# Attention with split operands: the row sum is made with exp, and V's lo part is read from PSUM between two groups of multiplications

## The chip, the cores and the metric

The kernel runs on one core of a Trainium2 chip. The metric is device time in microseconds (us) of one execution. Besides plain runs there is one profiled execution, from which all rows of a profile come. Engines are named PE (TensorE), DVE (VectorE), ACT (ScalarE), POOL (GpSimd) and SP (SyncE, which here only issues DMAs).

## The reference, cut to what matters

One transformer-like block on x of 2 x 2048 x 256, fp32: a layer norm, causal attention without heads, and a gated feed-forward part whose weights are -1, 0 or 1 with a scale; the results of both are added to x.

```
xn = layernorm(x)
q, k, v = xn @ Wq, xn @ Wk, xn @ Wv
scores = where(causal, einsum('bsd,btd->bst', q, k), -max)
attn = softmax(scores * dim_k ** -0.5)
out = x + (attn @ v) @ Wo + ffn(xn)      # ffn: 256 -> 1024 -> 1024 -> 1024 -> 256
```

## The kernel before, in words

**Precision.** An fp32 operand is split into a hi part, rounded to the fp32r format that TensorE multiplies, and a lo part, the rest. A product is hi x hi + hi x lo + lo x hi. Wv and Wo are multiplied together ahead (`wvo`), so V already holds V times Wo; Wq and Wk likewise (`wqk`).

**Tiling.** The sequences are cut into eight blocks of 512 rows, n = 0 to 3 of the first and 4 to 7 of the second. A tile (n, t) is 128 query rows. The 32 tiles run (3,3), (3,2) ... (0,0), then (4,0), (4,1) ... (7,3). Against the key block m a tile needs one score and one weighing; m runs up to n, where only t + 1 parts of 128 keys are wanted.

**`score`** (L344): TensorE multiplies q and k into a PSUM tile `ps` (six multiplications of 512 columns, L359), VectorE copies it to `s` and takes the maximum (L368). After a tile's last block VectorE makes `low`, the negated maximum (L374), ScalarE makes exp in place in pieces of up to 1024 keys with the sum of each piece (L380, `sums`), VectorE transposes 32 x 32 blocks inside 128 rows (L250), and SP stores the result to DRAM (`d`, L255).

**`turn`** (L404) gets P turned over: SP fetches the blocks in their new places (`e`, L262, four DMAs each, two buffers), ScalarE casts them to `pT`'s hi part (L418), and VectorE (even m) or GpSimd (odd m) makes the lo part (L420). Where a piece is short, TensorE transposes instead (L424). `pT` has four buffers and `turn` is written two blocks ahead of the use (`LEAD`).

**`weigh`** (L429): `po`, one PSUM bank of 2 x 256 fp32, gets in one go P's hi times V's hi (`po[:, 0, :]`) and P's hi times V's lo (`po[:, 1, :]`), one multiplication of 512 columns for each 128 keys (L438); then P's lo times V's hi is added to `po[:, 0, :]` with 256 columns each (L443). There are two `po` buffers. After the last block of a tile the sums are added up (L449), inverted (L451), ScalarE takes V's lo part out of PSUM times that (`y`, L453), and VectorE makes `r` = `po[:, 0, :]` x inv + y (L457). Four tiles make one store to DRAM (`r_d`, L462).

**Order.** `merged` (L43) alternates the scores of a tile with the weighing of earlier tiles by their costs; `beside` (L595) scatters in it the looks at the feed-forward weights (L516, L518, L523, L525: do the weights fit the exact ternary path?), which end in `flag` (L687). The framework's scheduler then moves instructions of each engine by its own estimates, and the order it leaves is fixed in the program: each engine works through its own in that order, waiting on semaphores. SP's DMAs too are in one such order. After attention the flag is read and the feed-forward part runs (L736 on), which is TensorE work nearly without gaps.

Of the kernel before, what the change touches and what calls it, by code (L numbers as in the profile page):

```python
# [9 lines left out]
F32 = mybir.dt.float32  # L10
# [4 lines left out]
AF = mybir.ActivationFunctionType  # L15
ALU = mybir.AluOpType
AX = mybir.AxisListType
# [3 lines left out]
P = 128  # L21
TB = 512
NT = TB // P
# [6 lines left out]
UK = 8  # L30
# [32 lines left out]
def attn_ffn_kernel(  # L63
# [35 lines left out]
    nc = tc.nc  # L99
    B, S, D = x.shape  # L100
# [6 lines left out]
    scale = float(wqT.shape[1] * P) ** -0.5  # L107
# [45 lines left out]
    with ExitStack() as actx:  # L153
# [3 lines left out]
        rp = actx.enter_context(tc.tile_pool(name="rp", bufs=2))  # L157
# [6 lines left out]
        small = actx.enter_context(tc.tile_pool(name="small", bufs=4))  # L164
# [82 lines left out]
        def turn_blocks(src, k, name):  # L247

            b = bp.tile([P, UK * P], F32, tag="b", name=f"b_{name}")[:, : k * P]
            nc.vector.transpose(  # L250
                b.rearrange("p (g k q) -> p k g q", g=P // Q, q=Q),
                src.rearrange("p (k g q) -> p k g q", g=P // Q, q=Q),
            )
            d = dram.tile([P, k * P], F32, name=f"d_{name}")
            nc.sync.dma_start(out=d, in_=b)  # L255
            return d
# [87 lines left out]
        def score(n, t, m, order):  # L344
            first = n - n % NB
            if m == order[0]:
                state[n, t] = {
                    "s": sp.tile([P, S], F32, tag="s", name=f"s_{n}_{t}"),
                    "tops": small.tile([P, NB], F32, tag="tops", name=f"tops_{n}_{t}"),
                    "sums": small.tile([P, NB], F32, tag="sums", name=f"sums_{n}_{t}", bufs=9),  # L350
                }
            st = state[n, t]
            w = TB if m < n else (t + 1) * P
            at = (m - first) * TB
            ps = ps_s.tile([P, TB], F32, tag="ps", name=f"pss_{n}_{t}_{m}")
            k = 0
            for c in range(DC):
                for a, b in ((0, 0), (0, 1), (1, 0)):
                    nc.tensor.matmul(  # L359
                        out=ps[:, :w], lhsT=qs[n][:, c, a, ts(t, P)], rhs=ks[m][:, c, b, :w],  # L360
                        start=(k == 0), stop=(m < n and k == 3 * DC - 1),
                    )
                    k += 1
            if m == n:
                nc.tensor.matmul(
                    out=ps[:, ds(w - P, P)], lhsT=ident_r, rhs=mask_r, start=False, stop=True
                )
            marks["DVE"] = nc.vector.tensor_scalar(  # L368
                st["s"][:, ds(at, w)], ps[:, :w], 1.0, None, ALU.mult, ALU.max,
                accum_out=st["tops"][:, m - first : m - first + 1],  # L370
            ).ins
            if m == order[-1]:
                low = small.tile([P, 1], F32, tag="low", name=f"low_{n}_{t}")
                nc.vector.tensor_reduce(  # L374
                    low, st["tops"][:, : n - first + 1], AX.X, ALU.max, negate=True
                )
                kt = (n - first) * NT + t + 1
                for u in range(0, kt, UK):
                    at = ds(u * P, min(UK, kt - u) * P)
                    marks["ACT"] = nc.scalar.activation(  # L380
                        st["s"][:, at], st["s"][:, at], AF.Exp, bias=low,
                        accum_out=st["sums"][:, u // UK : u // UK + 1],
                    ).ins
                for u in range(0, kt, UK):
                    k = min(UK, kt - u)
                    if by_blocks(n, t, first + u // NT):
                        d = turn_blocks(st["s"][:, ds(u * P, k * P)], k, f"{n}_{t}_{u}")
                        units.append((n, t, u, k, d))

        units, fetched = [], {}  # L390

        def by_blocks(n, t, m):
            kt = (n % NB) * NT + t + 1
            u = (m % NB) * NT // UK * UK
            return min(UK, kt - u) >= LEAST and (n, t) != (N - 1, NT - 1)
# [33 lines left out]
        def weigh(n, t, m):  # L429
            first = n - n % NB  # L430
            st = state[n, t]
            if m == first:
                st["po"] = ps_o.tile([P, 2, D], F32, tag="po", name=f"po_{n}_{t}")
            tiles = NT if m < n else t + 1
            pT = st.pop(m)

            for j in range(tiles):
                nc.tensor.matmul(  # L438
                    out=st["po"], lhsT=pT[:, 0, ts(j, P)], rhs=vs[m][:, j, :, :],
                    start=(m == first and j == 0), stop=False,  # L440
                )
            for j in range(tiles):
                nc.tensor.matmul(  # L443
                    out=st["po"][:, 0, :], lhsT=pT[:, 1, ts(j, P)], rhs=vs[m][:, j, 0, :],
                    start=False, stop=(m == n and j == tiles - 1),
                )
            if m == n:
                total = small.tile([P, 1], F32, tag="total", name=f"total_{n}_{t}")
                nc.vector.reduce_sum(total, st["sums"][:, : (n - first) * NT // UK + 1], axis=AX.X)  # L449
                inv = small.tile([P, 1], F32, tag="inv", name=f"inv_{n}_{t}")  # L450
                nc.vector.reciprocal(inv, total)  # L451
                y = rp.tile([P, D], F32, tag="y", name=f"y_{n}_{t}")
                nc.scalar.activation(y, st["po"][:, 1, :], AF.Copy, scale=inv)  # L453
                if n not in attn:
                    attn[n] = rp.tile([P, NT, D], F32, tag="r", name=f"r_{n}"), []
                r, made = attn[n]
                nc.vector.scalar_tensor_tensor(  # L457
                    r[:, t, :], st["po"][:, 0, :], inv, y, ALU.mult, ALU.add
                )
                made.append(t)  # L460
                if len(made) == NT:
                    nc.sync.dma_start(out=r_d[n], in_=r.rearrange("p t d -> p (t d)"))  # L462
                del state[n, t]

        def score_steps(n, t):
            order = list(range(n - n % NB, n + 1))
            return [
                (6 * (TB if m < n else (t + 1) * P), lambda m=m: score(n, t, m, order))
                for m in order
            ]  # L470

        def weigh_steps(g, until):

            steps = []
            while g < len(blocks) and blocks[g][0] <= until:
                while turned[0] <= min(g + LEAD, len(blocks) - 1) and (
                    turned[0] <= g or blocks[turned[0]][0] <= until + 1
                ):
                    b = blocks[turned[0]]
                    steps.append((0 if by_blocks(*b[1:]) else 2 * TB, lambda b=b: turn(*b[1:])))  # L480
                    turned[0] += 1
                _, n, t, m = blocks[g]
                steps.append((6 * TB if m < n else 6 * P * (t + 1), lambda b=blocks[g]: weigh(*b[1:])))
                g += 1
            return g, steps
# [43 lines left out]
        sums = xh0.rearrange("p c h t -> p (c h) t")  # L529
# [79 lines left out]
        queries(NB - 1, 1)  # L609
        order = list(range(NB - 1, -1, -1))  # L610
        score(NB - 1, NT - 1, NB - 1, order)
        wvo = weights_product("wvo", raw["v"], raw["o"], 1.0)
        for n in order[1:]:
            keys(n)
            score(NB - 1, NT - 1, n, order)
            for half in range(2):
                values(n + 1, half)
# [5 lines left out]
        tiles = [divmod(i, NT) for i in range(NB * NT - 1, -1, -1)]  # L623
# [37 lines left out]
        j = -1  # L661
# [460 lines left out]
```

## Time and profile before

| | us |
|---|---|
| Median of 3 runs | 874.41 (873.32 to 876.95) |
| The profiled execution, its own time | 872.97 |
| Its span, first to last instruction | 871.1 |
| PE busy | 851.1 (98%) |
| DVE, ACT, POOL busy | 630.3, 498.2, 236.3 |
| Attention on PE | until 276.9 of the span |

A busy share is the mean over stages. In a row of the costliest groups one reads line, engine, operation, tiles, shape and count, then busy time, mean ns of one, and the idle time ahead of it with what ended it. DMAs in flight don't show as busy time of an engine.

### The profile page before, as it was taken

The page shows a single profiled execution, that of the slowest core. Times are in us where ns is not written, and L with a number is a line of the kernel's source. Part 1 is how long each engine was busy: PE and PEld are TensorE (multiplying, and loading weights), DVE is VectorE, ACT ScalarE, POOL GpSimd, SP SyncE. Part 2 cuts the span into 40 slices and gives each one's busy share as a digit, 9 for nine tenths or more (in the row PEclk, how much of TensorE's full clock was granted, in tenths as well). Part 3 has the DMA queues.
Part 4 walks back from the last instruction along what each step waited for, and adds up shares of the span by engine and source line. Part 5 has one row for each costly group of instructions (what it writes and reads, how often), then busy time and mean ns, then how long its engine had stood idle before and what let it go on. Part 6 is the DMA issues. An engine that isn't in the chain of part 4 may idle for free.

```text
span 871.1 us, 12211 instructions
## 1 busy us (share of the span) xinstructions
PE 851.1 (98%) x4280; PEld 720.7 (83%) x4280; DVE 630.3 (72%) x1127; ACT 498.2 (57%) x881; POOL 236.3 (27%) x176
## 2 busy tenths in 40 slices
PE   8999999999989999999999999999999999999996
PEld 5888888988877878888988888988888898888886
DVE  5699688786873995985496596569478648848663
ACT  2547555755644665677266486536657635657670
POOL 4112633201111473540143150025024012402401
PEclk8999999999999999999999999999999999999999
DMA  9867599866792979743424444443444432144412
GB/s 322 312 230 226 176 326 300 298 230 212 243 324 93 375 280 336 273 146 143 139 87 150 146 144 145 149 127 103 145 145 145 146 139 97 49 145 146 145 49 77
DMA packets 63845, 162.51 MB, mean 187 GB/s; under 512 B 6560, under 2 KB 36384, under 8 KB 54560
## 3 DMA queue, kind: packets, MB, share of 16 engines
q1 hardware_dynamic: 58304, 145.92, 48.4%
q10 hardware_dynamic: 5472, 15.73, 5.6%
q8 instruction: 36, 0.59, 0.3%
q14 instruction: 33, 0.27, 0.1%
HBM read 120.21 MB, written 47.71 MB: 193 GB/s over the span
## 4 chain that ended last, share of the span: by engine, by line
PE 61%; DMA 3%; POOL 1%; DVE 1%; issue 0%; SPq 0%; DVEq 0%; POOLq 0%
PE ps_h_X L780 26%; PE ps_h_Z L780 13%; PE ps_w_B L736 10%; PE ps_h_Y L780 7%; PE ps_y L918 6%; DMA stgt_h<-in_ffn_h_w 1%; DMA w_h_S<-factors_h 1%; POOL sums_h L151 1%; DVE f_w_B L762 0%; DMA rt<-r_d 0%; POOL rt L908 0%; DVE h_B L720 0%; DMA out<-yt 0%; POOL f_w_B L761 0%; DVE f_w_B L742 0%
## 5 line engine op out<-in xcount | busy, mean ns | idle before, releaser
L359 PE MATMUL pss<-k,q 128*128 128x512 f32 (+3 forms) x480 | 110.4, 368 | 2.1 <-DVE q L210 1.1
L359 PEld LDWEIGHTS pss<-k,q 128*128 128x128 f32 x480 | 81.6, 189 | 14.9 <-DVE q L210 1.4
L780 PE MATMUL ps_h_X<-h_h_T,w_h_S 128*128 128x512 f32 x384 | 89.1, 389 | 0.3 <-DMA w_h_S<-factors_h 0.3
L780 PEld LDWEIGHTS ps_h_X<-h_h_T,w_h_S 128*128 128x128 f32 x384 | 72.0, 188 | 15.6 <-ACT k_h_u L801 0.7
L438 PE MATMUL po<-v,pT 128*128 128x512 f32 x272 | 79.0, 403 | 3.7 <-ACT pT L418 2.8
L420 POOL TENSOR_TENSOR pT<-e,pT 128x512 fp32r<-128x512 f32 (+3 forms) x30 | 35.6, 1188 | 161.6 <-ACT pT L418 111.0
L908 POOL TENSOR_TENSOR rt<-rt,xt 128x1024 f32<-128x1024 f32 x8 | 19.6, 2453 | 209.9 <-DMA rt<-r_d 209.9
L801 ACT ACTIVATE k_h_u<-k_h_u,h_s_sb 128x512 f32<-128x512 f32 x64 | 46.3, 724 | 41.1 <-DVE k_h_u L800 40.9
L741 ACT ACTIVATE f_w_B<-ps_w_B,w_s_sb 128x512 f32<-128x512 f32 x64 | 43.0, 684 | 43.5 <-PE ps_w_B L736 43.5
L918 PEld LDWEIGHTS ps_y<-w_sbt,h_h_B 128*128 128x128 f32 x512 | 62.0, 192 | 0.3
L918 PE MATMUL ps_y<-w_sbt,h_h_B 128*128 128x256 f32 x512 | 62.1, 283 | 0.0
L736 PE MATMUL ps_w_B<-xh,w_sb 128*128 128x512 f32 x256 | 59.5, 390 | 1.3 <-DVE r L457 1.3
L418 ACT CAST pT<-e 128x512 fp32r<-128x512 f32 (+3 forms) x60 | 32.6, 574 | 48.9 <-DMA e<-d 31.0
L780 PE MATMUL ps_h_X<-h_h_T,w_h_A 128*128 128x512 f32 x256 | 59.3, 389 | 0.0
L780 PE MATMUL ps_h_Y<-h_h_B,w_h_A 128*128 128x512 f32 x256 | 59.3, 389 | 0.0
L736 PE MATMUL ps_w_B<-xh1t,w_sb 128*128 128x512 f32 x256 | 58.7, 389 | 0.0
L438 PEld LDWEIGHTS po<-v,pT 128*128 128x128 f32 x272 | 48.6, 192 | 11.6 <-ACT pT L418 3.3
L736 PEld LDWEIGHTS ps_w_B<-xh,w_sb 128*128 128x128 f32 x256 | 47.8, 188 | 11.2 <-issue 1.5
L780 PEld LDWEIGHTS ps_h_Y<-h_h_B,w_h_A 128*128 128x128 f32 x256 | 48.0, 188 | 10.0
L780 PEld LDWEIGHTS ps_h_X<-h_h_T,w_h_A 128*128 128x128 f32 x256 | 48.0, 188 | 10.0
L736 PEld LDWEIGHTS ps_w_B<-xh1t,w_sb 128*128 128x128 f32 x256 | 48.0, 188 | 10.0
L380 ACT ACTIVATE s<-s,low 128x1024 f32<-128x1024 f32 (+7 forms) x48 | 43.0, 897 | 20.3 <-DVE low L374 19.9
(139 smaller groups left out, 1846.7 us busy)
## 6 DMA issues: line engine op xcount, KB each, us to landing
w_h_S<-factors_h SPq DMA_DIRECT2D x32, 1024.0 KB, 4.7
w_h_A<-factors_h SPq DMA_DIRECT2D x24, 1024.0 KB, 4.7
d<-b SPq DMA_DIRECT2D x18, 512.0 KB, 4.2
e<-d SPq DMA_DIRECT2D x72, 128.0 KB, 4.1
xT_d<-k SPq DMA_DIRECT2D x8, 1024.0 KB, 7.5
stg<-in_ffn_h_w ACTq DMA_DIRECT2D x16, 512.0 KB, 6.6
x<-in_attn_x SPq DMA_DIRECT2D x16, 256.0 KB, 5.5
r_d<-r SPq DMA_DIRECT2D x8, 512.0 KB, 5.3
```

Source lines behind the costliest of these rows:

```text
L151: engine.tensor_tensor(sums[:, i, :], x, y, op)
L359: nc.tensor.matmul(out=ps[:, :w], lhsT=qs[n][:, c, a, ts(t, P)], rhs=ks[m][:, c, b, :w], start=(k == 0), stop=(m < n and k == 3 * DC - 1),)
L380: marks["ACT"] = nc.scalar.activation(st["s"][:, at], st["s"][:, at], AF.Exp, bias=low, accum_out=st["sums"][:, u // UK : u // UK + 1],).ins
L418: nc.scalar.copy(hi, src)
L420: engine.tensor_tensor(lo, src, hi.bitcast(F32), ALU.subtract)
L438: nc.tensor.matmul(out=st["po"], lhsT=pT[:, 0, ts(j, P)], rhs=vs[m][:, j, :, :], start=(m == first and j == 0), stop=False,)
L736: nc.tensor.matmul(out=p, lhsT=w[:, c, ts(o, P)], rhs=xh[:, c, a, :], start=(c == 0 and a == 0), stop=(c == DC - 1 and a == 1),)
L741: nc.scalar.activation(f, p1, AF.Silu, scale=sc["w1"][:, o : o + 1])
L780: nc.tensor.matmul(out=out[o], lhsT=w[:, c, ts(o, P)], rhs=sets[right][c][:, a, :], start=(start and c == 0 and a == 0), stop=(c == HK - 1 ...
L801: nc.scalar.activation(C[k][o], r[o] if r else banks[o], AF.Gelu, scale=s[:, at : at + 1])
L908: nc.gpsimd.tensor_tensor(rest, rest, xt, ALU.add)
L918: nc.tensor.matmul(out=ys[t][:, :D], lhsT=h[c][:, a, ts(t, P)], rhs=w3_sb[:, c, :], start=(c == 0 and a == 0), stop=(c == HC - 1 and a == 1),)
```

## The change

The sum over the pieces and its reciprocal are written in `score`, right behind a tile's exp and block transposes, and the reciprocal is kept with the tile's state in one of nine buffers. In `weigh`, at the last block of a tile, ScalarE's y is written between the hi multiplications and the lo multiplications of that block, where it was written after both. The framework tracks `po` as one tile, so the lo multiplications that follow y in the text wait until y has been read. Both groups of multiplications get `skip_group_check=True`, since the bank is read while its accumulation is open. r stays the last step. As the scheduler places instructions anew, their order on every engine differs in the whole of attention; what is computed does not.

```diff
@@ score
                         units.append((n, t, u, k, d))
+                total = small.tile([P, 1], F32, tag="total", name=f"total_{n}_{t}")
+                nc.vector.reduce_sum(total, st["sums"][:, : (kt - 1) // UK + 1], axis=AX.X)
+                st["inv"] = small.tile([P, 1], F32, tag="inv", name=f"inv_{n}_{t}", bufs=9)
+                nc.vector.reciprocal(st["inv"], total)
@@ weigh
             for j in range(tiles):
                 nc.tensor.matmul(
                     out=st["po"], lhsT=pT[:, 0, ts(j, P)], rhs=vs[m][:, j, :, :],
-                    start=(m == first and j == 0), stop=False,
-                )
+                    start=(m == first and j == 0), stop=False, skip_group_check=True,
+                )
+            if m == n:
+                y = rp.tile([P, D], F32, tag="y", name=f"y_{n}_{t}")
+                nc.scalar.activation(y, st["po"][:, 1, :], AF.Copy, scale=st["inv"])
             for j in range(tiles):
                 nc.tensor.matmul(
                     out=st["po"][:, 0, :], lhsT=pT[:, 1, ts(j, P)], rhs=vs[m][:, j, 0, :],
-                    start=False, stop=(m == n and j == tiles - 1),
+                    start=False, stop=(m == n and j == tiles - 1), skip_group_check=True,
                 )
             if m == n:
-                total = small.tile([P, 1], F32, tag="total", name=f"total_{n}_{t}")
-                nc.vector.reduce_sum(total, st["sums"][:, : (n - first) * NT // UK + 1], axis=AX.X)
-                inv = small.tile([P, 1], F32, tag="inv", name=f"inv_{n}_{t}")
-                nc.vector.reciprocal(inv, total)
-                y = rp.tile([P, D], F32, tag="y", name=f"y_{n}_{t}")
-                nc.scalar.activation(y, st["po"][:, 1, :], AF.Copy, scale=inv)
                 if n not in attn:
                     attn[n] = rp.tile([P, NT, D], F32, tag="r", name=f"r_{n}"), []
                 r, made = attn[n]
                 nc.vector.scalar_tensor_tensor(
-                    r[:, t, :], st["po"][:, 0, :], inv, y, ALU.mult, ALU.add
+                    r[:, t, :], st["po"][:, 0, :], st["inv"], y, ALU.mult, ALU.add
                 )
```

## The prediction

> **What bounds the kernel now.** I read the busy shares first, then TensorE's own waits, the windows around its largest hole, the timeline there, and last the tile `po` that the change works on.
>
> ```profile
> PE 851.1 (98%) x4280; PEld 720.7 (83%) x4280; DVE 630.3 (72%) x1127; ACT 498.2 (57%) x881; POOL 236.3 (27%) x176
> ```
>
> TensorE bounds. Only its holes, or work added to it, move the end. Its waits, from the list of who waited for whom (engine, line, releaser: us in total, times, longest):
>
> ```profile
> PE po L438 <- ACT pT L418: 2.8, 1, 2.8
> ...
> PE ps_w_B L736 <- DVE r L457: 1.3, 1, 1.3
> ...
> PE po L438 <- DVE r L457: 0.9, 1, 0.9
> ```
>
> The windows (stretch, length, busy us of each engine, then TensorE's granted clock, DMA share, GB/s) divide attention from 53 us on:
>
> ```profile
> 53.00:240.00 187.00, 183.72 (x1029) 159.28 (x1028) 154.81 (x403) 113.03 (x228) 52.95 (x50) 1.00 0.77 249
> ...
> 257.20:261.00 3.80, 1.05 (x10) 0.81 (x8) 2.03 (x5) 1.89 (x5) 0.00 (x0) 0.98 0.88 279
> 261.00:264.50 3.50, 3.46 (x11) 2.93 (x12) 1.58 (x5) 2.48 (x5) 1.44 (x2) 0.54 0.33 91
> 264.50:278.20 13.70, 12.42 (x76) 10.68 (x74) 5.06 (x9) 4.67 (x9) 1.89 (x2) 1.00 0.05 14
> ```
>
> TensorE stands idle for 3.3, 2.75 and 1.3 us, and after the hole at 258 its clock is 0.54 for 3.4 us, worth 1.7 us. These 9 us are all that a better order inside attention could win. The feed-forward part after 278 us keeps its instructions. Now `po` (min/median/max ns) and who let ScalarE wait before y:
>
> ```profile
> L453 ACT ACTIVATE y<-po,inv x32: 452/469/489, 73.1 to 276.9; 128x256 f32<-128x256 f32 x32
> L457 DVE SCALAR_TENSOR_TENSOR r<-po,inv,y x32: 438/475/486, 76.4 to 277.4; 128x256 f32<-128x256 f32 x32
> ...
>   PE po L443: 14.2, 9
> ```
>
> Only before 9 of 32 y's did ScalarE sit waiting for TensorE. At most others y was late, because ScalarE was behind. One such place in the timeline of tile (2,2), whose last `po` multiplication started at 116.11:
>
> ```profile
> 116.11 0.52 PE L443 MATMUL po<-v,pT 128*128 128x256 f32 x3
> ...
> 120.45 1.06 ACT L523 ACTIVATE stg<-stg 128x1024 f32<-128x1024 f32 x1 [1.23 <-DMA stg<-in_ffn_h_w]
> 121.41 0.46 ACT L453 ACTIVATE y<-po,inv 128x256 f32<-128x256 f32 x1
> ```
>
> Pairing each y with its `po` in the timeline, y starts between 0.04 and 4.8 us after the last multiplication of its tile. Nobody on TensorE cares today.
>
> **What the Trainium skill says.** "PSUM — Partial Sum Buffer", Terms, calls simultaneous access by TensorE and ScalarE to one bank and quadrant an error. `po` is one whole bank of 512 fp32, so a y read between hi and lo must hold lo back; in the built program each last lo group indeed waits for ScalarE. No run here shows the collision. "TensorE: Matmul & The Clock Gate", Architectural detail, calls ScalarE and VectorE strict FIFO; the y above, ready at 116.7 and started at 121.4 behind other work, agrees. The same page, Part 1, halves the clock after about one idle window of 3.4 us; here 2.8 us of idle were followed by 0.54.
>
> **The change, part by part.**
>
> *Sum and reciprocal with exp.* 32 x (114 + 153) ns = 8.5 us of VectorE stay. In both built programs each sum stands right after its tile's last block transpose, which waits for the same exp; on the tiles without transposes it stands near where it stood. Only the reciprocal moves, past one to six VectorE instructions. No TensorE wait hangs on it. Cost: 0. If the cover went (a sum blocking VectorE on a late exp), it would show as the 1.1 us in 3 waits that these sums have now, doubled: +1 us at most.
>
> *y before lo.* Same 32 activations and 544 `po` multiplications. What is new is 32 waits: lo of a tile's last block waits for y, y for the hi group and for everything ahead of it on ScalarE. Behind lo, on TensorE, everything queues. From the timeline, spacings are 0.227 us (512 columns), 0.12 (256) and 0.11 (128). A wait with nothing between hi and lo costs: end of the last hi 0.39 us after its start, handover 0.05, y 0.47, handover 0.05 = 0.96 instead of 0.23, so 0.73 us. The built order leaves three tiles so: (7,0), (7,1), (7,3). In the other 29, other multiplications stand between, 2.0 to 7.1 us by those spacings, median about 4.3. Bounds for these 29: below, 0, y always in time. Above, adding to each tile today's lateness of y and 1 us for lo, y and handovers, eight tiles exceed their cover, by 9.4 us together. But in the new order ScalarE's y stands ahead of work that it stood behind (at (2,3) two passes of 1.05 us, at (2,2) an exp of about 1 us and a pass that had waited for a DMA), so most of that lateness goes. What remains is casts that wait for their transfer (31.0 us in 16 waits, 1.9 each): if four of them outlast their cover by 0.5 us, +2 us. I take +2.
>
> *What the later lo moves.* The pT ring has four buffers, so a last block's pT is freed later, the casts behind it come later, the e buffers (two) are read later, and SP's fetches into them start later. SP's queue shows it: at the end e_1_0, e_1_8, e_2_0 and e_2_8 all stand behind the last d stores and the flag's load stands ahead of e_2_0; before, e_1_0 stood ahead of those stores and the flag behind every fetch. I walked this tail from E, the end of score (7,3),5, with 29.4 us of multiplications left. Before, 276.9 - 29.4 - 4.7 of stalls puts E at 242.8.
> - TensorE reaches lo of (7,0),4 at E+8.7. Its VectorE subtraction stands behind the mask of the last w3 tile (L516). That load took 7.0 us (251.88 to 258.9); issued at E+2.1 it ends at 9.1, then 0.69 + 0.69: E+10.5. TensorE waits 1.9.
> - That subtraction frees e for e_1_0: issued at 10.5, before at 244.61, E+1.8. Its second half stands behind the store of r, which waits for the subtraction, a weight look (1.25), another subtraction and r: last issue 13.8, landing 4.1 later (median of these fetches), cast 0.62: (7,1),4 starts at 18.5. TensorE, with y of (7,0) uncovered, is there at 15.5: 3.0 idle.
> - e_2_0 waits for GpSimd's subtraction of (7,1),5 (20.4), last issue 21.9, 2.3 to land (the quiet-queue value), cast: 24.8. TensorE arrives at 24.1. e_2_8 then fits.
> - From 24.8: 5.2 + 5.6 + 0.9 of multiplications and transposes and 0.7 for (7,3): E+37.2 against 34.1. Afterwards r follows lo without y, -0.5.
> Sum 2.6; with part of a half-clock phase after the 3.0 us hole, +3. Ends: -4.5 (hole and phase gone) to +7 (each fetch 2 us slower).
>
> *Sum.* 0 + 2 + 3 = +5 us. The profiled execution took 872.97 (span 871.1 and 1.9 around it), hence 878; the median of the runs is 1.4 above that, hence 879.4.
>
> **Rivals.**
> - *Hidden anyway.* ScalarE is 57% busy, the order puts 4 us between hi and lo, and the many waits of TensorE on casts and subtractions in 53 to 240 us leave only 3.3 us idle. Then only the three uncovered y's remain (0.73 twice, and 0.73 - 0.5 at the end, where r no longer waits for y), less about 1 us of the present hole: 874.4 + 1.5 + 0.2 - 1 = 875. Against: the tail's fetches stand visibly later.
> - *The tail gets shorter* (faster). In the new order 8 us more multiplications follow the last scores: at the point that has 17.8 us left before, the new one has 26. If DMAs return quickly (2.3 us each, the w3 load within 5), (7,1),4 finds its cast nearly ready, the 2.75 us hole and the 1.7 us of half clock go, and r is quicker by 0.5: 874.4 - 4.9 = 869.5. It decides where e_1_0 has landed by E+14.
> - *ScalarE sets the pace.* Casts that wait for e, exp that waits for VectorE's maxima (15.9 us in 12 waits), then y: the full 9.4 of shortage with the tail: 874.4 + 9.4 + 5 = 889. It needs y to stay as late as today.
> - *The change does nothing, as the sums stand where they stood.* True of the sums; the lo waits are in the built program.
>
> **Chances.** Slower by lo's waits and tail 0.46 (own range 877 to 884), ScalarE's pace 0.07, hidden 0.33, shorter tail 0.14. About 0.5% (4.4 us) is what a measurement here tells from no change. So slower 0.53, same 0.33, faster 0.14. The range 870 to 886 drops about half of the shorter tails and the slowest of the pace cases.
>
> **What would show it.** Right: L443 waiting for ScalarE's y at several places, about 0.7 us each at (7,0), (7,1); holes of 2 to 3 us before `po` L438 near E+15, waiting for ScalarE's cast, itself for e; VectorE waiting for the stg load ahead of it; span about 876. Wrong: no PE wait on y at all, TensorE busy without a hole from 240 to 278, or granted clock 1.00 throughout the tail. The prediction fails if the new order's DMA traffic lands faster than today's, or if an earlier stretch loses or gains several us that I took as unchanged.

## The result, and the profile after

| | before | after |
|---|---|---|
| Median, timed side by side | 873.66 us | 879.43 us |
| Ratio, 95% interval | | 1.0076 (1.0053 to 1.0099) |
| The profiled execution, its span | 872.97, 871.1 | 878.6, 876.7 |
| Feed-forward part begins (first multiplication into `ps_w_B`) | 278.16 | 283.15 |
| From there to the end | 592.9 | 593.6 |

The change makes the kernel 0.76% slower; the forecast was 879.4 us. The forecast's sum was right for a reason that was only half right: of its two losses one was hardly there, and the other was larger.

Here as in the prediction (7,1),4 stands for tile (7,1) against key block 4, and e_1_0 for the buffer into which SP fetches the turned blocks of tile (7,1) for its first 1024 keys (e_1_8: the rest). In the kernel after, lines are numbered a little higher: the cast to `pT` is L422, the subtraction L424, hi of `po` L443, lo L451, y L449, r L459, the mask of a weight look L518, the first feed-forward multiplication L738. TensorE's busy share and its waits, which answer to those shown of before (engine, line, releaser: us in total, times, longest):

```profile
PE 854.5 (97%) x4280; PEld 721.7 (82%) x4280; DVE 630.7 (72%) x1127; ACT 498.3 (57%) x881; POOL 236.0 (27%) x176
```

```profile
PE po L443 <- ACT pT L422: 2.8, 3, 1.6
PE po L451 <- DVE pT L424: 1.8, 1, 1.8
PE po L451 <- ACT y L449: 1.8, 3, 0.7
...
PE ps_w_B L738 <- DVE r L459: 0.8, 1, 0.8
```

The second and third lines are new: lo waits once for a subtraction on VectorE, and three times for y. The first was one hole of 2.8 us and is three smaller ones. The windows, with the columns as before:

```profile
53.00:240.00 187.00, 184.23 (x1020) 159.45 (x1019) 156.23 (x410) 112.35 (x224) 49.05 (x49) 0.99 0.78 256
242.00:250.00 8.00, 8.00 (x44) 6.81 (x43) 5.33 (x17) 4.45 (x9) 1.36 (x1) 1.00 1.02 353
250.00:262.00 12.00, 8.05 (x39) 6.45 (x38) 5.58 (x10) 4.73 (x10) 2.44 (x2) 0.83 0.41 125
262.00:284.00 22.00, 19.83 (x102) 16.09 (x103) 7.34 (x11) 6.97 (x14) 5.48 (x4) 0.94 0.19 50
```

The last two stretches before, the second up to the feed-forward part:

```profile
250.00:262.00 12.00, 9.21 (x49) 7.79 (x48) 7.68 (x20) 6.79 (x13) 2.38 (x3) 0.95 0.92 271
262.00:278.20 16.20, 14.92 (x84) 12.78 (x82) 5.93 (x11) 6.15 (x13) 2.69 (x3) 0.93 0.10 29
```

From 53 to 240 us TensorE is as busy as before (184.2 of 187 us, before 183.7). The loss lies behind 250: 4 idle us in 12 and a clock of 0.83 (before 2.8 and 0.95), then 2.2 idle us (before 1.3). The tile `po`:

```profile
L449 ACT ACTIVATE y<-po,inv x32: 453/473/483, 72.1 to 281.0; 128x256 f32<-128x256 f32 x32
L459 DVE SCALAR_TENSOR_TENSOR r<-po,inv,y x32: 442/476/487, 79.0 to 282.4; 128x256 f32<-128x256 f32 x32
...
  PE po L443: 17.0, 7
```

Now ScalarE sits waiting for the hi group before 7 of 32 y's, before it was 9: ScalarE is still late at most tiles. But at 29 of them TensorE has something else to do. To place the loss, both traces were read at the same point of TensorE's work. With 29.3 us of multiplications left before the feed-forward part (the point E of the prediction) before stands at 242.6 us and after at 242.9. From there to the feed-forward part it takes 35.6 us before and 40.3 after: 4.7 of the 5.6 us between the spans are in this tail, 0.3 ahead of it and 0.6 behind. A second profile of the kernel after (span 879.9) agrees on the place: of 8.8 us above before 7.6 are in the tail.

The tail in the timeline of TensorE, after (start, us, engine, line, operation, count, then idle time and releaser):

```profile
253.37 0.74 PE L451 MATMUL po<-v,pT 128*128 128x256 f32 x4 [1.84 <-DVE pT L424]
...
259.82 0.36 PE L451 MATMUL po<-v,pT 128*128 128x256 f32 x1 [0.54 <-ACT y L449]
261.75 2.07 PE L443 MATMUL po<-v,pT 128*128 128x512 f32 x4 [1.57 <-ACT pT L422]
...
268.67 0.47 PE L451 MATMUL po<-v,pT 128*128 128x256 f32 x2 [0.66 <-ACT y L449]
...
281.57 0.74 PE L451 MATMUL po<-v,pT 128*128 128x256 f32 x4 [0.56 <-ACT y L449]
283.15 1.16 PE L738 MATMUL ps_w_B<-xh,w_sb 128*128 128x512 f32 x4 [0.84 <-DVE r L459]
```

The three y's are those of (7,0), (7,1) and (7,3), the three that the built order had left uncovered. The idle times are 6.0 us here and 4.05 before (2.75 and 1.3): 2.0 of the 4.7. The y's add 1.8 and the subtraction 1.8, while the hole ahead of (7,1),4 is 1.2 shorter than before's and the last wait for r 0.4. TensorE's clock was at half from 254.5 and from 261.3, for 3.4 us each, before only once, from 260.8: 1.7. The remaining 1.0 is put down to what each of the four additional stops costs beside its idle time (behind a stop four multiplications of 512 columns take 1.20 us, otherwise 1.09); it was not measured apart.

What was late ahead of this, in the timelines of ScalarE, VectorE, GpSimd and SP, after:

```profile
246.75 1.16 ACT L380 ACTIVATE s<-s,low 128x1024 f32<-128x1024 f32 x1 [3.55 <-DVE low L374]
...
249.03 0.60 ACT L422 CAST pT<-e 128x512 fp32r<-128x512 f32 x1
```

```profile
250.95 0.69 DVE L518 TENSOR_SCALAR stg<-stg 128x1024 uint32<-128x1024 uint32 x1 [1.44 <-DMA stg<-in_ffn_w_w]
251.56 1.76 DVE L424 TENSOR_TENSOR pT<-e,pT 128x512 fp32r<-128x512 f32 x1
```

```profile
251.18 1.59 POOL L424 TENSOR_TENSOR pT<-e,pT 128x512 fp32r<-128x512 f32 x1 [7.39 <-ACT pT L422]
```

```profile
243.81 10.35 SPq L262 DMA_DIRECT2D e<-d  x6
256.89 0.34 SPq L464 DMA_DIRECT2D r_d<-r  x1
257.27 10.03 SPq L262 DMA_DIRECT2D e<-d  x14
```

ScalarE waited 3.55 us for the negated maximum of the last tile, (7,3), then took its exp, and only then, at 249.03, cast the first block of (7,0), which stood behind it. So the lo part of (7,0),4 came late on VectorE, and e came free late for e_1_0. Its first two fetches are the last two of the row of six, issued at 253.38; the store of r stands next in SP's queue, and the other two fetches came behind it from 257.27. The last of the four had landed at 261.0, 18.1 us past E. Before, e_1_0 had landed at 252.2, 9.7 past E.

One more thing is in these lines. The subtraction at 251.56 took 1.76 us where such a one takes 0.69, and GpSimd's subtraction ran until 252.77. The Trainium skill, "SBUF — State Buffer", SBUF: two separate sides, says that VectorE and GpSimd share a pair of ports under an exclusive lock, and that a VectorE operation with two SBUF inputs waits for a GpSimd operation on SBUF that started first. The trace agrees: the four VectorE subtractions of 512 columns with both inputs in SBUF that began with 0.8 to 1.2 us of a GpSimd subtraction to go took 1.38 to 1.76 us, and each ended 0.55 us behind GpSimd's; most others took 0.67 to 0.69. So of the 1.84 us wait above an estimated 1.07 (1.76 less 0.69) belongs to this lock and not to the mask that the prediction named.

### The profile page after: what moved, and what is told of

Read it like the earlier page. It is cut to its first block, busy times and chain, and to the rows that moved or that the text cites. A ratio compares the mean times of both kernels' runs of the same rounds, so it can differ in the third digit from the quotient of the medians.

```text
span 876.7 us, 12246 instructions
## 1 busy us (share of the span) xinstructions
PE 854.5 (97%) x4280; PEld 721.7 (82%) x4280; DVE 630.7 (72%) x1127; ACT 498.3 (57%) x881; POOL 236.0 (27%) x176
## 4 chain that ended last, share of the span: by engine, by line
PE 61%; DMA 3%; POOL 1%; DVE 1%; issue 0%; SPq 0%; DVEq 0%; POOLq 0%
PE ps_h_X L782 26%; PE ps_h_Z L782 12%; PE ps_w_B L738 10%; PE ps_h_Y L782 7%; PE ps_y L920 6%; DMA stgt_h<-in_ffn_h_w 1%; DMA w_h_S<-factors_h 1%; POOL sums_h L151 1%; DVE f_w_B L764 0%; DMA rt<-r_d 0%; POOL rt L910 0%; DVE h_B L722 0%; DMA out<-yt 0%; POOL f_w_B L763 0%; DVE f_w_B L744 0%
## 5 line engine op out<-in xcount | busy, mean ns | idle before, releaser
L443 PE MATMUL po<-v,pT 128*128 128x512 f32 x272 | 79.0, 405 | 3.7 <-ACT pT L422 2.8
L424 POOL TENSOR_TENSOR pT<-e,pT 128x512 fp32r<-128x512 f32 (+3 forms) x30 | 36.7, 1225 | 159.7 <-ACT pT L422 80.3
L738 PE MATMUL ps_w_B<-xh,w_sb 128*128 128x512 f32 x256 | 59.5, 390 | 0.8 <-DVE r L459 0.8
L738 PE MATMUL ps_w_B<-xh1t,w_sb 128*128 128x512 f32 x256 | 58.7, 389 | 0.0
L443 PEld LDWEIGHTS po<-v,pT 128*128 128x128 f32 x272 | 48.8, 193 | 11.8 <-ACT pT L422 3.3
L738 PEld LDWEIGHTS ps_w_B<-xh,w_sb 128*128 128x128 f32 x256 | 47.8, 188 | 10.8 <-issue 1.0
L738 PEld LDWEIGHTS ps_w_B<-xh1t,w_sb 128*128 128x128 f32 x256 | 48.0, 188 | 10.1 <-issue 0.2
L763 POOL TENSOR_TENSOR k_h_u<-k_h_p,k_h_u 128x512 f32<-128x512 f32 x16 | 24.3, 1522 | 109.8 <-ACT h_h_B L721 97.4
```

Source lines behind the costliest of these rows:

```text
L424: engine.tensor_tensor(lo, src, hi.bitcast(F32), ALU.subtract)
L443: nc.tensor.matmul(out=st["po"], lhsT=pT[:, 0, ts(j, P)], rhs=vs[m][:, j, :, :], start=(m == first and j == 0), stop=False, skip_group_che ...
L738: nc.tensor.matmul(out=p, lhsT=w[:, c, ts(o, P)], rhs=xh[:, c, a, :], start=(c == 0 and a == 0), stop=(c == DC - 1 and a == 1),)
L763: nc.gpsimd.tensor_tensor(B["B12"][i], B["B22"][i], B["B12"][i], ALU.subtract)
```

## The experiments

The theory after the comparison: the loss is in the tail, by the later order of casts and fetches and by y's without cover. The rival: y between hi and lo costs something at every tile, through 32 waits of lo. Another: any new order on the engines costs a few us by chance. Later one more stood against these: that the transfers beside the 1 MB load of xh are what is late. In the lists below "above before" is against runs of the kernel before on the same chip.

**One half of the change: sums early, y behind lo.**

```diff
@@ weigh (against the kernel after)
-            if m == n:
-                y = rp.tile(...); nc.scalar.activation(y, st["po"][:, 1, :], AF.Copy, scale=st["inv"])
             for j in range(tiles):
                 nc.tensor.matmul(out=st["po"][:, 0, :], ...)
             if m == n:
+                y = rp.tile(...); nc.scalar.activation(y, st["po"][:, 1, :], AF.Copy, scale=st["inv"])
```

> The sum and the reciprocal stand in score as in the changed kernel, y stays behind both groups of multiplications as before; the sixteen other tiles of the order hardly move. Late-tail theory (the lo groups held back by y free the pT buffers late, so the last fetches of e start late): no change, 873.7 within 1.5, with one hole of about 2.8 us ahead of po near the end as before. Rival of the waits on y: no change either. Rival of the shuffle (any new order on the engines costs a few us by chance): 875 to 879.

Measured: 874.35 us, before 872.9, ratio 1.0024 (1.0006 to 1.0043). This is in the range of the late tail and under that of chance. The order of the tail is that of before (the last scores stand where they stood), and its hole is 2.3 us. The early sums alone cost 0.1 to 0.4%. The profiled execution (872.6, 1.8 under the median of these runs) has a tail 2.3 us longer than before's, of which 0.6 is idle time and 1.7 a second half-clock phase. One execution does not tell whether the loss lies there: its place stays open.

**The other half: y early, sums back in the weighing.**

```diff
@@ score
-                total = ...; nc.vector.reduce_sum(total, ...); st["inv"] = ...; nc.vector.reciprocal(st["inv"], total)
@@ weigh, behind hi
             if m == n:
+                total = ...; nc.vector.reduce_sum(total, ...); st["inv"] = ...; nc.vector.reciprocal(st["inv"], total)
                 y = rp.tile([P, D], F32, tag="y", name=f"y_{n}_{t}")
```

> The kernel after, with sum and reciprocal back in the weighing, just ahead of y, which stays between hi and lo. Nothing is left out. Theory: the place of the sums is worth nothing and y between hi and lo is the whole loss: 4.5 to 7 us above before, TensorE waiting for y at the three tiles of block 7. Rival: making the sums early is what the y needs to be in time, and without it y comes later at more tiles: TensorE waits for y at more than three tiles and the time is 8 us or more above before. Other rival: with this kernel's order of the tail (4 us less of multiplications behind the last scores than in the kernel after) the tail loses less: 2 to 4 us above before.

Measured: 873.7 us, before 875.16, ratio 0.9997 (0.9983 to 1.0011): no loss. All three expectations missed, the last by the least. All 32 y's stand between hi and lo here, and TensorE waits for two of them (0.4 us at 136.6, 0.56 at (7,3)). Its waits:

```profile
PE po L439 <- ACT pT L418: 3.9, 3, 2.3
...
PE po L451 <- DVE pT L420: 1.0, 1, 1.0
...
PE po L451 <- ACT y L449: 1.0, 2, 0.6
```

What differs is the order that the scheduler left. Two lines of ScalarE and one of SP:

```profile
251.07 0.30 ACT L418 CAST pT<-e 128x128 fp32r<-128x128 f32 x1 [2.20 <-DVE low L374]
251.28 1.15 ACT L380 ACTIVATE s<-s,low 128x1024 f32<-128x1024 f32 x1
```

```profile
247.86 1.94 SPq L262 DMA_DIRECT2D e<-d  x4
```

The exp of (7,3), which begins at 251.28, stands behind all casts of (7,0), of which the first line is the last, and the four fetches of e_1_0 go out together at 247.86. They have landed 12.9 us past E, and the tail takes 35.9 us, as before (it idles 1.0 us more than before's and has no half-clock phase). So y ahead of lo need not cost anything, and a new order need not either. With both halves together the scheduler puts the last scores, with their exp, ahead of work that the tail needs sooner: in the kernel after 8.7 us more of multiplications are left behind those scores than before, here 4.7. But this kernel's order differs from both others in all of attention, so the run does not single out the place of that exp.

**y early in all blocks but the last.**

```diff
@@ weigh, behind hi (and y behind lo for the others)
-            if m == n:
+            if m == n and n < N - 1:
```

> The changed kernel, but in the last query block, tiles (7,0) to (7,3), y goes back behind lo. The order at the end is that of the changed kernel: 27.9 us of multiplications left at the last score, the fetches e_0_8 to e_2_8 behind the last stores of d. No multiplication of block 7 waits for y. Late-tail theory: most of the loss stays, +3.5 to +4.5 against before, 877 to 878.5, with the hole ahead of (7,1),4. Rival of the waits on y: the 1.8 us of waits and what they bring are gone, 874 to 875.5.

Measured: 876.95 us, before 872.9, ratio 1.0045 (1.0025 to 1.0064). The 4 us above before are in the range of the late tail. With 28 early y's and the order of the kernel after, TensorE waits for no y at all, so in this profile those 28 have no direct cost. Its hole at (7,1),4 became larger instead:

```profile
PE po L443 <- ACT pT L422: 5.1, 2, 3.8
```

The three uncovered y's of block 7 are worth about 0.3%, 2 to 2.5 us, of the loss (the interval of the kernel after, 1.0053 to 1.0099, overlaps this one). The rest stays, and the largest wait of the tail is the hole before the casts of e_1_0, which here had landed 16.6 us past E.

**y early in the last block alone**, the other way round.

```diff
-            if m == n:
+            if m == n and n == N - 1:
```

> y ahead of lo only in tiles (7,0) to (7,3), sums in score. The order at the end is that of before: 19.2 us left at the last score, e_1_0 ahead of the last stores of d. Late-tail theory: close to before, 873.7 to 875.2, the waits on y at most 0.7 us each at one or two places. Rival of the waits on y: 875.5 to 877, since the same last tiles wait for y as in the changed kernel.

Measured: 875.6 us, ratio 1.0032 (1.0015 to 1.0048), 2.7 us above before. One y is waited for (0.6 us), the hole for the casts is 2.1. Its profiled execution has half clock in another place too (at 125.9 us for 3.4 us), behind a wait of the scores on VectorE's q (1.7 us). The time lies in the range of the rival and not in that of the late tail: for the late tail this is a miss. But one wait of 0.6 us for y is not what the rival counted on. The order here is nearly that of the run with the early sums alone, and the two ratios (1.0024 and 1.0032) are not told apart, so what the early sums cost may be all of it.

**The kernel after with one look less**, so that VectorE does not wait for the last w3 tile. The second half of w3 isn't looked at, which leaves out one mask, one pass and its part of the flag.

```diff
@@ the looks at w3
-            if c >= 2:
+            if c == 2:
```

> The changed kernel without the look at the second half of w3 (its load, the mask on VectorE, the sum on ScalarE are left out; the flag then does not cover those weights). It takes away what VectorE waits for ahead of the subtraction of (7,0),4. Late-tail theory: the chain of fetches starts up to 1.8 us earlier and one half-clock phase less, so 2 to 4 us faster than the changed kernel, 875.5 to 877.5. Rival: the fetch is bound by e's readers on GpSimd anyway, then at most 1 us.

Measured: 879.29 us, ratio 1.0077 (1.0048 to 1.0106): nothing gained, a miss for the late tail and in the range of the rival. The wait of lo of (7,0),4 was gone, and TensorE came to (7,1),4 3.9 us earlier, at 256.3, but there it stood 2.4 us longer:

```profile
260.25 2.07 PE L443 MATMUL po<-v,pT 128*128 128x512 f32 x4 [3.95 <-ACT pT L422]
```

It then ran 6.8 us at half clock where after had 3.4 twice. So the stall on the mask was not on the path that sets the end. VectorE's subtraction took 1.77 us here as well, beside GpSimd's, and e_1_0 could go out only 0.56 us earlier, at 252.82.

**The store of r one weighing later**, so that all of e_1_0 stands ahead of it in SP's queue.

```diff
@@ weigh, last block of a tile
+                for w in held: w()
+                held.clear()
-                    nc.sync.dma_start(out=r_d[n], in_=r.rearrange("p t d -> p (t d)"))
+                    held.append(lambda n=n, r=r: nc.sync.dma_start(out=r_d[n], in_=...))
+                    if n in (0, N - 1): held.pop()()
```

> The kernel after, with the store of a block of r written one weighing later, so that in SP's queue all four fetches of e_1_0 stand ahead of it (and two or three of e_1_8). Nothing is left out. Theory, the late tail: in the kernel after, the second half of e_1_0 was issued at 257.27, 3.5 us after the first half, because the store of r stood between and r was made only at 256.37; it landed at 260.7 and the cast, at 261.08, let TensorE wait 1.57 us and then run 3.4 us at half clock. Without the store between, the second half is issued near 254.5 and lands near 257, ahead of TensorE: the hole before (7,1),4 and its half clock go, 1.6 + 1.7 = 3.3 us, so 2 to 3.5 us faster than after: 2.5 to 4 us above the kernel before. Rival: GpSimd's subtraction and the d loads set the landing of the whole e_1 group and the hole stays: within 1 us of after, 5.5 to 6.5 above before.

Measured: 879.21 us, before 875.16, ratio 1.0051 (1.0028 to 1.0073), 4.05 us above before: just outside the range of the theory, under that of the rival. The mechanism is there: e_1_0 lands 15.4 us past E instead of 18.1, and the hole shrinks from 1.57 to

```profile
258.13 1.20 PE L443 MATMUL po<-v,pT 128*128 128x512 f32 x4 [0.59 <-ACT pT L422]
```

The profiled tail takes 38.4 us, 1.9 less than after; but that execution is the fastest of the seven, 3.3 us under their median. By the times alone it isn't told from after, as the intervals overlap.

**The load of xh behind the last fetch of e**, in the kernel before and in the kernel after.

```diff
@@ fetch_blocks
-                nc.sync.dma_start(out=e[ts(g, Q), :]...)
+                marks["SP"] = nc.sync.dma_start(out=e[ts(g, Q), :]...).ins
@@ after the attention loop
-        nc.sync.dma_start(out=xh0...)
+        with tc.issue_after(marks["SP"]):
+            nc.sync.dma_start(out=xh0...)
```

> The kernel before, with the load of xh (the 1 MB that the feed-forward part starts with) issued behind the last fetch of e instead of at 241.7 us. Nothing is left out. Theory, transfers share the DMA engines: in the kernel before the e fetches issued at 244.6 beside xh landed 6 us later, and those issued at 262.3 in a quiet queue 2 us later. With xh gone the fetches and the w3 load of 244 to 258 land 2 to 4 us earlier, the hole of 2.75 us at 258 and its half clock (1.7 us) go or shrink: 1.5 to 4.5 us faster than the kernel before. Rival: the waits are those of the order (e buffers, subtractions, SP's queue) and not of the transfers' length: within 1 us of before.

> The kernel after, with the same move of the load of xh behind the last fetch of e; the scheduler then also puts the store of r behind all of e_1_0, as in the run with the later store. Nothing is left out. Theory, the late tail made of both the transfers' length and the store in SP's queue: the 1.84 us wait of lo of (7,0),4 on the subtraction behind the mask of w3 (whose load landed at 250.95 beside xh) and the 1.57 us hole at (7,1),4 both go, with both phases of half clock; what stays are the three uncovered y's: 4 to 6.5 us faster than after, 0 to 2 above before. Rival: only the order of lo counts (pT and e buffers come free too late): 0 to 2 us faster than after.

Measured: in the kernel before 875.06 us against 875.16, ratio 1.0008 (0.9991 to 1.0024): nothing. In the kernel after 877.46, ratio 1.0033 (1.0017 to 1.0049), 2.3 us above before. The first answers the question of the transfers: in the order of before the 1 MB beside the fetches doesn't set the time (the hole was 2.75 us before; the profile of this run, 3.2 us above its median, has two, of 3.0 and 1.8). The second, between its two expectations, gave back more than half of the loss, though here the scheduler also put the store of r behind all of e_1_0. The hole at (7,1),4 was still 1.70 us; the wait of (7,0),4 on VectorE was gone, and 0.55 us on GpSimd had come in its place.

**The exp of the last tile behind the casts of (7,0) and the first of (7,1)**, one edge of order more in the kernel after; and that kernel again beside it.

```diff
@@ turn
-                nc.scalar.copy(hi, src)
+                marks["CAST"] = nc.scalar.copy(hi, src).ins
@@ score
+                    with tc.issue_after(marks["CAST"]) if (n, t) == (N - 1, NT - 1) else nullcontext():
                         marks["ACT"] = nc.scalar.activation(st["s"][:, at], st["s"][:, at], AF.Exp, ...)
```

> The kernel after with one order edge more: ScalarE's exp of the last tile, (7,3), is kept behind the casts of (7,0) and the first of (7,1), where the scheduler had put it ahead of all casts of (7,0). Sums, y and lo stay as in the kernel after, and the last scores stand as early in TensorE's order. Nothing is left out. Theory, the order on ScalarE: in the kernel after ScalarE stood 3.55 us before that exp, waiting for VectorE's low, and then took 2.3 us for it, with the casts of (7,0) queued behind; so e was freed for e_1_0 at 253.4, 10.5 us after the last score of 512 columns before (E), against E+1.8 to E+5.2 in the kernel before and in the one with late sums, which lose nothing. With the exp behind the casts e_1_0 is issued by E+6, the wait on VectorE's subtraction (1.84) and the hole at (7,1),4 (1.57) go with their half clock, y of (7,0) is covered again: 4 to 6.5 us faster than after, 0 to 2 us above before. Rival: the loss comes from y standing in the way of lo and of the pT ring, and the exp's place is worth nothing: within 1.5 us of after, 5 to 7 above before.

> The kernel after, unchanged, timed beside the run with the last exp later. Both theories: 5.8 us above before (ratio 1.005 to 1.010), spans by the profile 874 to 878, as runs of one kernel differ in how much half clock the start has.

Measured: with the edge 877.01 us, ratio 1.0050 (1.0033 to 1.0067); after again 880.23, ratio 1.0069 (1.0041 to 1.0097); before 873.64. So 3.2 us of 6.6 came back by the medians, and 1.7 of 6.0 by the ratios, whose intervals overlap. The time lies between the theory and the rival. The kernel after was again as slow as expected; its profiled span, 879.9, was above the expected 874 to 878. The profile with the edge shows why only part came back. The first fetch of e_1_0 went out 6.8 us past E instead of 10.5, and all four landed by 11.2 instead of 18.1, sooner than in the kernel that loses nothing; the wait on VectorE's subtraction in the tail was gone. Not all of that is the exp's: the scheduler here also put the store of r behind these fetches, as in the run with the later store. And the moved exp is late for someone else: TensorE transposes P of (7,3) itself and stood for it,

```profile
255.79 1.09 PE L430 MATMUL pt<-ident,s 128*128 128x128 f32 x8 [0.86 <-ACT s L382]
```

and two y's of block 7 (0.66 and 0.56 us in its tail) were still uncovered.

**That edge and xh's load last.**

> The run with the last exp later, and with the load of xh behind the last fetch of e. Nothing is left out. If what is left of the tail's hole is the length of the transfers beside xh: 1 to 3 us faster than with the last exp later alone, and at or up to 2 us below the kernel before. If not, as the kernel before with that load moved (1.0008): within 1 us of the run with the last exp later alone.

Measured: 878.9 us, ratio 1.0052 (1.0032 to 1.0071): by the ratio the same as with the edge alone, by the median 1.9 us slower, and in no case faster. The transfers' length is not what is left.

**That edge, and y behind lo in block 7.**

> Both edits that each gave back part of the loss: the exp of (7,3) behind the casts of (7,0), and y behind lo in the four tiles of block 7. In the 28 tiles before, y stays between hi and lo. Nothing is left out. Theory, two separate pieces in the tail, the uncovered y's (0.3% given back without them) and the exp ahead of the casts (0.2% given back without it): together they give back 0.4 to 0.6 of the 0.7%: ratio to the kernel before 1.001 to 1.003, 1 to 2.5 us above it, no wait of TensorE on y, and the tail from E takes 35.5 to 37 us. Rival: both edits remove the same wait, and the rest of the loss lies ahead of E: ratio 1.004 to 1.005, 3.5 to 4.5 us above before.

Measured: 877.46 us, before 874.36, ratio 1.0028 (1.0013 to 1.0043): in the range of the two separate pieces by the ratio (by the medians 3.1 us above before, where 1 to 2.5 was expected), and below both measurements of the kernel after (1.0069 and 1.0076). No y is waited for, as expected, but the tail takes 38.3 us, where 35.5 to 37 was expected. A wait of the edge's own stands in it:

```profile
254.27 0.62 ACT L424 CAST pT<-e 128x512 fp32r<-128x512 f32 x1 [4.43 <-DMA e<-d]
254.80 1.14 ACT L382 ACTIVATE s<-s,low 128x1024 f32<-128x1024 f32 x1
```

```profile
256.09 1.97 PE L430 MATMUL pt<-ident,s 128*128 128x128 f32 x8 [2.94 <-ACT s L382]
```

The exp now stands behind the first cast of (7,1), ScalarE waits 4.43 us for that cast's fetch, and TensorE 2.94 us for the exp (2.6 in the run with xh later too). An exp just one cast earlier was not tried.

All profiled executions side by side: the tail from E to the feed-forward part, and the landing of e_1_0, which is the last of the 16 updates that the trace has for its fourth fetch:

| kernel | e_1_0 landed, past E | tail, us | ratio to before |
|---|---|---|---|
| before | 9.7 | 35.6 | 1 |
| y early, sums late | 12.9 | 35.9 | 0.9997 |
| before, xh last | 8.6 | 37.9 | 1.0008 |
| sums early, y late | 10.9 | 37.9 | 1.0024 |
| last exp later, y not in block 7 | 12.6 | 38.3 | 1.0028 |
| y only in block 7 | 9.7 | 37.5 | 1.0032 |
| after, xh last | 15.7 | 37.4 | 1.0033 |
| y not in block 7 | 16.6 | 38.0 | 1.0045 |
| last exp later | 11.2 | 37.3 | 1.0050 |
| after, store later | 15.4 | 38.4 | 1.0051 |
| last exp and xh later | 12.1 | 39.6 | 1.0052 |
| after, again | 18.6 | 43.2 | 1.0069 |
| after | 18.1 | 40.3 | 1.0076 |
| after, one look less | 16.8 | 40.5 | 1.0077 |

A single profiled tail varies by some 3 us, in part with the half-clock phases: 40.3 and 43.2 for the kernel after. The ends of the table are apart; its middle is sorted by neither column.

No kernel was faster than the kernel before. The one with early y and late sums is not told from it.

## Why the prediction was right, and where not

*Sum and reciprocal: 0.* Nearly so. The sums alone gave 1.0024, 0.1 to 0.4%, whose place was not found. What the step missed besides: together with the early y their place changes the scheduler's order of the tail; without them the early y costs nothing. In the second profile of the kernel after TensorE also stood 1.4 us at 135.05 for VectorE, which had just ended an r and a reciprocal; which of the two it was is not told. Five more kernels with this order had that wait, of 0.25 to 1.2 us; the first profile has none.

*y before lo: +2.* Here a step failed. It took 2 us for casts that outlast their cover at some of the 29 covered tiles. In the kernel after TensorE waits for y three times, at the three uncovered tiles; with y late in block 7 alone it waits for none. In its second profile, and in three kernels with its order, it waits once more, 0.2 to 0.5 us at one tile near 135 us. So the 29 cost 0 to 0.5 us together. The cover, 2.0 to 7.1 us of other multiplications, was enough for the 0.47 us of y and the queue ahead of it; the lower bound of that step was close to the value. The price of an uncovered tile, 0.73 us, was right: 0.54, 0.66 and 0.56 idle and some tenths for the stop. But (7,1)'s was listed as uncovered and then left out of the sum.

*What the later lo moves: +3.* The mechanism was right: e_1_0 was forecast to be issued at E+10.5 and E+13.8 at the last and (7,1),4 to start at E+18.5; it was 10.5, 14.9 and 18.9. The stall of lo of (7,0),4 was 1.84 us against 1.9. Under-sized was the end: 40.3 - 35.6 = 4.7 us. The walk had a hole of 3.0 and part of one half-clock phase; there were two phases, one of them right behind the stall of 1.84 us. That slowed TensorE on its way to (7,1),4, so the hole there was only 1.57. The forecast of 0.7 idle at (7,2),4 did not come. The named causes were partly wrong: a stall that the walk gave to the mask of w3 was in part VectorE's subtraction waiting for GpSimd's, and without that mask nothing was gained. That the stall had the forecast length was luck: the mask began at E+8.1, a microsecond sooner than in the walk, and the subtraction took a microsecond longer.

*The sum.* 0 + 2 + 3 = 5 us, measured 5.6 between the profiled executions and 5.8 between the medians. An error of +2 and one of about -2 met: that the sum came so close was luck.

*The rivals.* "Hidden anyway" was right, but for half a microsecond, for 29 of 32 y's and wrong for the tail. "The tail gets shorter" asked for e_1_0 landed by E+14; it came at 18.1. ScalarE never set the pace. That the change does nothing fell with the result.

What is shown: in both profiles most of the loss lies in the tail; the y's of block 7 hold 2 to 2.5 us of it; with all y's early and another order there is no loss. That the exp of (7,3) ahead of (7,0)'s casts makes e_1_0 late is shown by its first fetch, which went out 3.7 us sooner with the exp moved; the landing came 6.9 us sooner with the store of r out of the way too. But the time gave back only a quarter to a half, and with the y's of block 7 late as well, ratio 1.0028, a third or more of the loss was still there. How that rest divides between the edge's own waits, the early sums (0.24%) and anything ahead of E is open.

## What to carry to other kernels

A read of PSUM put between two groups that accumulate into it cost next to nothing in this kernel where other multiplications stood between them, and 0.5 to 0.7 us of idle time where none did: so look at the built order tile by tile, above all in the last block, where nothing is left to fill in. When two small edits cost little or nothing alone and more together, look at what each engine does last in the order that came out, at an in-order engine that waits for one thing (here 3.55 us for a maximum) with the work of the critical chain queued behind it. And a stall taken away ahead of a later wait may just lengthen that wait (here 1.57 us became 3.95), so follow the chain to its end before counting it.

## What was not expected of the hardware

- Half clock after short holes. The Trainium skill, "TensorE: Matmul & The Clock Gate", Part 1, speaks of one idle window of about 3.4 us. Here 1.84 us of idle time ending at 253.4 were followed by half clock from 254.5, and stalls of 0.98 and 0.59 us at 108.7 and 110.6 by one from 111.1. In the second profile of the same kernel the same two stalls (0.96 and 0.59) were not followed by one, and with y early and sums late a hole of 2.34 us was not either. All phases in attention lasted 3.4 or 6.8 us, so each costs an estimated 1.7 or 3.4.
- What decides seems to be how the holes fall on a fixed grid. Within each trace all phases begin whole multiples of 3.413 us apart. With TensorE's idle time summed in each cell of that grid, from 25 to 300 us in all fourteen traces, the 19 cells that were followed by a new half-clock phase had 1.55 to 3.3 us idle. Of the roughly 1000 other cells at full clock only two had as much (1.55 and 1.75). This is read from the traces and was not tested by a run. It fits the cases above: the 2.34 us hole lies across two cells.
- A VectorE subtraction of 512 columns took up to 1.76 us instead of 0.69 when one of GpSimd was running.
